# Four moves in the program's order, and sums of squares in exact bf16 parts, in a four-layer graph and expert network

## The chip, the cores and the metric

The kernel runs on one core of a Trainium2 chip. The metric is device time in microseconds (us) from start to end of one launch; lower is better. A core has four compute engines that run their own queues of instructions side by side: TensorE (PE in the profile: matmuls, and weight loads as PEld), VectorE (DVE), ScalarE (ACT) and GpSimd (POOL). SyncE (SP) issues most DMA transfers, POOL some. Each queue is executed in its order; engines wait for each other through semaphores. TensorE multiplies a stationary operand, loaded first, by a moving one.

## The reference, cut to what matters

1250 tokens of 512 features go through four layers. Each adds to x a graph part and a mixer part, both of the normed x, and then an expert part.

```python
for layer in 0..3:
    xn = layernorm(x)
    x = x + gnn[layer](xn, edges) + mixer[layer](xn)
    x = x + experts[layer](layernorm(x))

# layer 0, graph: h = xn @ W.T + b;  out[col] += dis[row]*dis[col] * h[row];  relu
# layer 0, mixer: twice an attention with random features, then an MLP
def softmax_kernel(data, proj, is_query, eps=1e-4):
    data_dash = (data * d**-0.25) @ proj.T                       # 64 -> 256 features, per head
    diag = sum(data**2, -1) * 0.5 * d**-0.5                      # the sum of squares per head
    m = max(data_dash, -1 if is_query else (-2, -1))
    return ratio * (exp(data_dash - diag - m) + eps)

# layer 1, graph: mean over neighbours @ W_l.T + xn @ W_r.T, batch norm over tokens, relu, + xn
# layer 1, mixer: linear attention, softmax over q's features
# layer 2, experts: two of eight for each token
h1 = rmsnorm(gelu(xf @ w1[e])) * n1[e]
h2 = rmsnorm(gelu(h1 @ w2[e])) * n2[e]
expert_out = (h2 + h1) @ w3[e]
# layer 3, mixer: XW_v = X @ W_v.T;  mean(XW_v over tokens) + X @ ((X @ W_theta.T).T @ XW_v) / (n*sqrt(d))
```

## The kernel before, in words

The tokens lie in 10 tiles of 125 rows; feature-major tensors (`xnT`, `kT`, `qT`) lie with 128 features on the partitions and are worked in chunks of 500, 500 and 250 tokens. `mm` writes a product of several terms to one of the PSUM banks that `bank()` gives out in turn; `transposed` turns a tile on TensorE against `ident`. The program is written in the order in which the work is wanted; a planner in the language reorders instructions on the engines by its own estimates, except those marked with `keep_in_program_order`. Pools reuse memory: what is opened later can lie where a closed pool lay, and then waits for the last readers of that memory.

Layer 0, front. `load_x` brings x in five transfers of two tiles, then `l0_front` loads W. For each tile it makes the layer norm (`ln_one`), a second norm `z` of it, turns both, and multiplies the tile before (`before`) with W; `hs` receives the product plus bias. Meanwhile `Graph.__init__` makes a tile `zero` on VectorE out of x0 (so that it waits for x) and POOL writes it in 29 DMAs over the DRAM adjacency table `adj` and a part of `yd`. x0 and `zero` lie in the pool `l0n`, which is closed after the front.

`Graph.start` makes one number (source, destination) of each edge, and `Graph.add`, 16 times, loads a row of these (`keyrow`, two buffers, on SP's queue), compares it on VectorE in ten operations `same`, and adds ten columns of counts to `adj` by indirect DMA. These groups are spread by the planner over the attention.

Layer 0, attention (`l0_attention`, run twice). Keys in four steps `keys(c)`, two heads each: project into `kT` in three chunks, square (`sq`), and sum the squares per head: a matmul with the squares as stationary operand and `halves`, a 128 x 2 constant of 0.5, as moving one. Then products with the projection `pj`, a maximum on VectorE, exponentials on ScalarE, and products with the weighted values `vw`. The pool of a keys stage, `kv`, holds `v`, `kT`, `sq`. Queries: `projected` makes `qT` and its squares a chunk ahead, `features_q` sums squares and makes features.

Layer 1. After the SAGE product (`over`), the four blocks `f` of the self product and the batch norm, `att.out` starts with `q_start` for two tiles (product with `wq`, softmax on ScalarE and VectorE), then loops over the tiles.

Layer 2, experts. A load is one expert's weight with one or two tiles of 128 slots. There are 28 loads in six groups of two stages here (`second` and `third`): for each load, scale `h` and turn it on TensorE, make `h1T` or `sT` out of that on VectorE, then multiply with w2 or w3.

Layer 3, mixer. Gram matrix of `xnT`, `half` = gram times wv in four blocks whose copies alternate between VectorE and ScalarE, then `tot`, the sum of `xnT` over tokens on VectorE, spread to `totb` and multiplied with wv for the mean. The planner is free to place `tot`; it put it ahead of the gram copies.

Of the kernel before, what the change touches and what calls it, by code (L numbers as in the profile page):

```python
# [8 lines left out]
F32 = mybir.dt.float32  # L9
# [48 lines left out]
def gps_d4_kernel(ctx: ExitStack, tc: tile.TileContext, a: dict, out: bass.AP):  # L58
# [22 lines left out]
    def load_x(engine, o):  # L81
        for t in range(0, NT, 2):
            move(engine, o[:, t:t + 2, :], a["x"][t * TP:(t + 2) * TP, :].rearrange("(t p) d -> p t d", p=TP))

    cols = const.tile([P, NCOL], F32, name="cols")
    nc.sync.dma_start(cols, a["cols"])
# [9 lines left out]
    halves = const.tile([P, 2], F32, name="halves")  # L96
# [94 lines left out]
    def ln_one(o, src, t, between=lambda: None):  # L191

        st = S.small.tile([TP, 6], F32, tag="st1", name="st1", bufs=4)
        nc.vector.bn_stats(st, src[:, t, :])
# [351 lines left out]
    class Graph:  # L546
# [4 lines left out]
        def __init__(self, pool, first, x):  # L551
            self.pool = pool
            self.next = 0

            nc.vector.tensor_scalar(first, x[:, 7:, :].rearrange("p t d -> p (t d)")[:, :T], 3e38, 0.0,
                                    op0=OP.is_gt, op1=OP.is_lt)
# [7 lines left out]
            self.count = pool.tile([TP, EC], F32, name="count")  # L564
            self.cell = pool.tile([TP, EC], I32, name="cell")
# [208 lines left out]
    def l0_front(pool, x0, xn, hs):  # L774


        w = load_w(a["L0_gnn_W"])
        b = row_bc(a["L0_gnn_b"])
        yT = xnT
        before = None  # L780
        for t in range(NT + 1):
            if t < NT:
                mv = ln_one(xn[:, t, :], x0, t)
# [7 lines left out]
                xnTt = S.small.tile([P, NC, TP], F32, tag="xnTt", name="xnTt")  # L791
                nc.scalar.copy(xnTt, transposed(xn[:, t, :]))
                gained(yT, t, transposed(z), ("L0_mix_ln1_g", "L0_mix_ln1_b", 0))
            if before is not None:
                u, m = before
                ps = bank()
                mm(ps[:TP, :], [(m[:, c, :], w[:, c, :]) for c in range(NC)])
                nc.vector.tensor_tensor(hs[:, u, :], ps[:TP, :], b[:TP, :], op=OP.add)
            before = t, xnTt
# [15 lines left out]
    RATIO = 256.0 ** -0.5  # L815

    def l0_attention(pool, i, xm, yT, front, then, aside=lambda: None):
# [17 lines left out]
        with tc.tile_pool(name=f"kv{i}", bufs=1) as kp:  # L835
# [20 lines left out]
            def keys(c):  # L856
# [6 lines left out]
                for c0, cn in CH:  # L863
                    sq = kp.tile([P, 500], F32, tag="sq", name="sq", bufs=2)
                    nc.scalar.activation(sq[:, :cn], kT[:, c0:c0 + cn], AF.Square)
                    for t, o in tiles_of(c0, cn):
                        mm(ps[:TP, 2 * t:2 * t + 2], [(sq[:, o:o + TP], halves)])
# [108 lines left out]
        with tc.tile_pool(name=f"q{i}", bufs=1) as qp:  # L976
# [4 lines left out]
            def features_q(qT, sq, at):  # L981
                psd = bank()
                for c in range(NC):
                    mm(psd[:TP, 2 * c:2 * c + 2], [(sq[:, c, at], halves)])
# [61 lines left out]
            def projected(o, c0, cn):  # L1046
                for c in range(NC):
                    proj_T(wq, c, c0, cn, o[0][:, c, :cn], "L0_mix_bq")
                    nc.scalar.activation(o[1][:, c, :cn], o[0][:, c, :cn], AF.Square)
# [5 lines left out]
            for k in range(len(CH) + 1):  # L1055
                if k < len(CH):

                    ahead.append([qp.tile([P, NC, 500], F32, tag=n, name=n, bufs=2) for n in ("qT", "sq")])
# [62 lines left out]
    def layer0_mixers():  # L1121
# [3 lines left out]
        with tc.tile_pool(name="l0a", bufs=1) as pool:  # L1125
            xn = nat(pool, "xn")
            hs = nat(pool, "hs")
            with tc.tile_pool(name="l0n", bufs=1) as lp:
                x0 = nat(lp, "x0")
                load_x(nc.sync, x0)  # L1130
                zero = lp.tile([TP, T], F32, name="zero")
                graph = Graph(gpool, zero, x0)
                yT, z = l0_front(pool, x0, xn, hs)
# [130 lines left out]
    class LinearAttention:  # L1264
# [25 lines left out]
        def out(self, pool, wq, use):  # L1290


            ready = [self.q_start(pool, t, wq) for t in range(2)]
# [88 lines left out]
    def layer1_mixers():  # L1382
        scales = dram.tile([T, 1], F32, name="scales")
        with tc.tile_pool(name="l1x", bufs=1) as pool:
# [48 lines left out]
            over(rows, False, more)  # L1433
            hT = pool.tile([P, NC, T], F32, tag="n1", name="hT")
            for f in range(NC):
                st = S.small.tile([P, 5, 6], F32, tag="bst", name="bst")
# [16 lines left out]
            rscope.close()  # L1453
# [36 lines left out]
            with tc.tile_pool(name="l1o", bufs=1) as op:  # L1490
                att.out(op, wq, use)
                arrival[1].step(NT)
# [117 lines left out]
    def layer2_ffn():  # L1610
# [4 lines left out]
        with tc.tile_pool(name="l2o", bufs=1) as op:  # L1615
# [29 lines left out]
            with tc.tile_pool(name="l2e", bufs=1) as pool:  # L1645
# [16 lines left out]
                class Group:  # L1662
# [26 lines left out]

                    def second(self):  # L1690
# [3 lines left out]
                        for i, (o, tiles) in zip(self.loads, self.at):  # L1694
# [6 lines left out]
                            for k in range(2):  # L1701
                                nc.vector.tensor_scalar(self.h1T[:, k, o * SL:(o + n) * SL], pt[:, k, :], n1[:, k:k + 1], None,
                                                        op0=OP.mult)
                            ps = bank()
# [5 lines left out]
                            for j in range(o, o + n):  # L1710
                                square(self.h2[:, j, :], ss[:, j:j + 1])
# [209 lines left out]
```

## Time and profile before

| | us |
|---|---|
| median of three runs | 3118.99 (3117.23 to 3127.1) |
| the profiled execution | 3127.68 |
| its span | 3125.7 |
| mean granted TensorE clock in it | 0.956 of full |
| TensorE busy | 2882.9 (92%) |
| VectorE busy | 1175.9 (38%) |
| ScalarE busy | 693.8 (22%) |
| POOL busy | 670.2 (21%) |

The profile shows one execution, here 8.7 us longer than the median. Its page gives busy times, 40 equal slices of the span (78 us each) in tenths, and groups of instructions by line, engine and operands; the timeline gives start and duration of each and, in brackets, how long the engine stood idle before it and what released it. L182 is the line of `mm`, L188 that of `transposed`.

### The profile page before, as it was taken

What the parts mean: (1) busy time and instruction counts of PE and PEld (TensorE: products, weight loads), DVE (VectorE), ACT (ScalarE), POOL (GpSimd) and SP (SyncE); (2) the same over time, 40 slices, a digit from 0 to 9 for tenths busy, and PEclk for the clock granted to TensorE, in tenths of its full rate; (3) what the DMA queues carried; (4) which work ended last, traced back from release to release, by engine and by line L of the source; (5) the groups of instructions that cost most, each with busy time, mean ns of one, the idle gap of its engine ahead of it and who ended that gap; (6) DMA issues with size and microseconds to landing.
All of it is one profiled execution on the core that took longest, in us unless ns stands there. A gap on an engine that the chain in (4) does not pass through costs nothing. (4 is left out here: it accounts for less than half of the span.)

```text
span 3125.7 us, 31412 instructions
## 1 busy us (share of the span) xinstructions
PE 2882.9 (92%) x11531; PEld 1724.7 (55%) x11531; DVE 1175.9 (38%) x2812; ACT 693.8 (22%) x1469; POOL 670.2 (21%) x492
## 2 busy tenths in 40 slices
PE   8999999999999999999899979999799979789884
PEld 4457744455576444656455556766454547345562
DVE  6835511143355323344531550001443135362433
ACT  3133311132233122110321431111241013230010
POOL 3444444442001300133310011000301002022023
PEclk9999999999999999999899989999899989999987
DMA  7411111121001200237310017775210026430086
GB/s 229 118 15 15 17 28 31 28 31 14 14 14 40 82 27 27 80 108 249 88 34 1 21 44 283 254 252 176 82 41 1 8 73 193 159 104 10 24 312 201
DMA packets 234382, 275.70 MB, mean 88 GB/s; under 512 B 104352, under 2 KB 131600, under 8 KB 234210
## 3 DMA queue, kind: packets, MB, share of 16 engines
q1 hardware_dynamic: 123841, 185.13, 18.3%
q0 software_dynamic: 96832, 63.67, 8.9%
q10 hardware_dynamic: 13536, 24.65, 2.1%
q8 instruction: 102, 1.67, 0.2%
q14 instruction: 71, 0.57, 0.1%
HBM read 228.04 MB, written 44.91 MB: 87 GB/s over the span
## 5 line engine op out<-in xcount | busy, mean ns | idle before, releaser
L182 PE MATMUL ps<-xnT,w 128*128 128x500 f32 (+1 forms) x1536 | 554.8, 516 | 2.9 <-PEq L698 2.3
L182 PE MATMUL ps<-w,hT 128*125 128x512 f32 (+1 forms) x1232 | 542.1, 592 | 0.9 <-ACT hT L1246 0.9
L182 PEld LDWEIGHTS ps<-xnT,w 128*128 128x128 f32 x1536 | 289.4, 190 | 252.0 <-issue 239.7
L620 POOL DMA_INDIRECT adj<-count,cell x160 | 319.7, 1998 | 369.5 <-DMA adj<-count,cell 338.1
L182 PEld LDWEIGHTS ps<-w,hT 128*125 128x125 f32 (+1 forms) x1232 | 228.9, 189 | 270.3 <-issue 260.8
L182 PE MATMUL ps<-w,xnT 128*125 128x512 f32 x560 | 254.7, 604 | 0.0
L182 PE MATMUL ps<-xgT,w 128*128 128x256 f32 (+1 forms) x1256 | 234.0, 344 | 2.8 <-issue 2.8
L182 PEld LDWEIGHTS ps<-xgT,w 128*128 128x128 f32 x1256 | 207.5, 193 | 43.5 <-issue 22.2
L378 POOL DMA_INDIRECT xg<-rows,r_idx x94 | 89.7, 955 | 571.5 <-PE ps L419 289.1
L208 DVE TENSOR_TENSOR xn<-ps,xn 125x512 f32<-125x512 f32 x100 | 69.0, 690 | 348.3 <-PE ps L182 348.3
L523 ACT ACTIVATE hT<-ps,cols 128x500 f32<-128x500 f32 (+1 forms) x108 | 65.6, 608 | 478.2 <-PE ps L182 478.1
L182 PEld LDWEIGHTS ps<-w,xnT 128*125 128x125 f32 x560 | 103.4, 192 | 115.4 <-issue 114.6
L439 POOL DMA_INDIRECT came<-yd,slots x80 | 100.5, 1256 | 302.1 <-SPq L408 136.3
L420 DVE COPY xgT<-ps 128x512 f32<-128x512 f32 x94 | 62.0, 687 | 246.3 <-PE ps L419 225.0
L182 PE MATMUL ps<-hs,AT 125*125 125x512 bf16 x600 | 134.3, 382 | 4.2 <-PEq L698 4.2
L182 PE MATMUL ps<-AT,n 125*128 125x500 bf16 (+1 forms) x720 | 127.2, 339 | 0.0
L429 DVE TENSOR_TENSOR y<-ps,erow 128x512 f32<-128x512 f32 x71 | 49.1, 692 | 194.6 <-PE ps L182 187.3
L182 PEld LDWEIGHTS <-AT 125*125 125x125 bf16 x600 | 82.0, 138 | 51.8 <-issue 7.8
L1532 ACT ACTIVATE hT<-ps,b 128x256 f32<-128x256 f32 (+1 forms) x112 | 48.8, 436 | 262.1 <-PE ps L182 262.1
L182 PEld LDWEIGHTS <-n 125*128 125x128 bf16 x720 | 70.1, 97 | 58.0 <-issue 1.1
L925 PE MATMUL ps<-ex,vw 125*65 125x256 f32 x320 | 83.3, 411 | 2.8 <-DVE vw L911 2.8
L208 DVE TENSOR_TENSOR x<-ps,x 125x512 f32<-125x512 f32 x50 | 34.5, 691 | 130.4 <-PE ps L182 117.1
(404 smaller groups left out, 3651.2 us busy)
## 6 DMA issues: line engine op xcount, KB each, us to landing
w<-in_L_ffn_we_dram SPq DMA_DIRECT2D x56, 1024.0 KB
w<-in_L_ffn_w_dram SPq DMA_DIRECT2D x58, 512.0 KB
yd<-y ACTq DMA_DIRECT2D x94, 256.0 KB
w<-in_L_mix_W_dram SPq DMA_DIRECT2D x16, 1024.0 KB
w<-in_L_ffn_w_dram SPq DMA_DIRECT2D x44, 256.0 KB
rows<-z SPq DMA_DIRECT2D x40, 224.0 KB
keyrow<-keys SPq DMA_DIRECT2D x16, 546.9 KB
erow<-in_L_ffn_b_dram SPq DMA_DIRECT2D x30, 256.0 KB
```

The costliest lines, as they stand in the source:

```text
L182: nc.tensor.matmul(o, l, r, start=(i == 0), stop=(i == n - 1))
L208: nc.vector.tensor_tensor(dst, ps, dst, op=OP.add)
L378: nc.gpsimd.indirect_dma_start(g, None, self.rows, bass.IndirectOffsetOnAxis(ap=self.idx[:, t:t + 1], axis=0))
L420: nc.vector.tensor_copy(xgT[:, :, j * SL:(j + 1) * SL], ps.rearrange("p (c s) -> p c s", c=NC))
L429: nc.vector.tensor_tensor(y, ps, bias, op=OP.add)
L439: nc.gpsimd.indirect_dma_start(y, None, yd, bass.IndirectOffsetOnAxis(ap=slots[n][:, k * NT + t:k * NT + t + 1], axis=0))
L523: nc.scalar.activation(hT[:, f, :cn], ps[:, :cn], act, bias=b1(f))
L620: nc.gpsimd.indirect_dma_start(adj, bass.IndirectOffsetOnAxis(ap=self.cell[:, c:c + 1], axis=0), self.count[:, c:c + 1], None, compute_op= ...
L925: nc.tensor.matmul(self.ps[j][:C + 1, :NB], self.vw[j][:, t, :], self.ex[k][:, j, u, :], start=(t == 0), stop=(t == NT - 1))
L1532: nc.scalar.activation(hT[f // NC][:, f % NC, :ns], ps[:, :ns], AF.Gelu, bias=b1[:, f:f + 1])
```

## The change

Five edits:

1. Front of layer 0: x comes in two single tiles, then W, then pairs of tiles, with the constants `cols` after the first pair; the product lags two tiles, and `xnTt` has three buffers; tile 2's first norm instruction is kept in program order; `zero` and the clearing of `adj` and `yd` move into `Graph.clear`, called at the sixth tile.
2. Layer 1: `q_start` for two tiles moves ahead of the last block `f`.
3. Layer 2: in `second` and `third` the next load is turned and scaled ahead of this load's product.
4. Layer 3: `tot` is kept in program order, behind the copies of `half`.
5. Layer 0, attention: each square is split into three bf16 numbers whose sum it is, and `halves` is bf16, so that a sum is three bf16 matmuls in place of one f32.

```diff
             engine.dma_start(o[r], i[r])
-    def load_x(engine, o):
-        for t in range(0, NT, 2):
-            move(engine, o[:, t:t + 2, :], a["x"][t * TP:(t + 2) * TP, :].rearrange("(t p) d -> p t d", p=TP))
+    def load_x(engine, o, tiles=range(0, NT, 2), n=2):
+        for t in tiles:
+            move(engine, o[:, t:t + n, :], a["x"][t * TP:(t + n) * TP, :].rearrange("(t p) d -> p t d", p=TP))
     cols = const.tile([P, NCOL], F32, name="cols")
-    nc.sync.dma_start(cols, a["cols"])
     ident = const.tile([P, P], F32, name="ident")
...
     nc.vector.memset(eps6, 1e-6)
-    halves = const.tile([P, 2], F32, name="halves")
+    halves = const.tile([P, 2], BF16, name="halves")
     nc.vector.memset(halves, 0.0)
...
         return ps[:, :NC * TP].rearrange("p (c t) -> p c t", t=TP)
-    def ln_one(o, src, t, between=lambda: None):
+    def ln_one(o, src, t, between=lambda: None, in_order=False):
         st = S.small.tile([TP, 6], F32, tag="st1", name="st1", bufs=4)
-        nc.vector.bn_stats(st, src[:, t, :])
+        ins = nc.vector.bn_stats(st, src[:, t, :])
+        if in_order:
+            tc.keep_in_program_order(ins)
         mv = S.small.tile([TP, 4], F32, tag="mv1", name="mv1", bufs=4)
...
-        def __init__(self, pool, first, x):
+        def __init__(self, pool):
             self.pool = pool
             self.next = 0
-            nc.vector.tensor_scalar(first, x[:, 7:, :].rearrange("p t d -> p (t d)")[:, :T], 3e38, 0.0,
-                                    op0=OP.is_gt, op1=OP.is_lt)
+            self.count = pool.tile([TP, EC], F32, name="count")
+            self.cell = pool.tile([TP, EC], I32, name="cell")
+        def clear(self, first, x):
+            tc.keep_in_program_order(nc.vector.tensor_scalar(first, x[:, 7:, :].rearrange("p t d -> p (t d)")[:, :T], 3e38, 0.0,
+                                    op0=OP.is_gt, op1=OP.is_lt))
             for t in range(NT):
...
                 nc.gpsimd.dma_start(yd[r:r + n, :], first[:n, :D])
-            self.count = pool.tile([TP, EC], F32, name="count")
-            self.cell = pool.tile([TP, EC], I32, name="cell")
         def start(self, z):
...
                 self.some()
-    def l0_front(pool, x0, xn, hs):
-        w = load_w(a["L0_gnn_W"])
+    def l0_front(pool, x0, xn, hs, w, aside):
         b = row_bc(a["L0_gnn_b"])
         yT = xnT
-        before = None
-        for t in range(NT + 1):
+        before = []
+        for t in range(NT + 2):
+            if t == 6:
+                aside()
             if t < NT:
-                mv = ln_one(xn[:, t, :], x0, t)
+                mv = ln_one(xn[:, t, :], x0, t, in_order=t == 2)
                 r = S.small.tile([TP, 2], F32, tag="r2", name="r2", bufs=4)
...
                 nc.vector.tensor_scalar(z, xn[:, t, :], r[:, 1:2], None, op0=OP.mult)
-                xnTt = S.small.tile([P, NC, TP], F32, tag="xnTt", name="xnTt")
+                xnTt = pool.tile([P, NC, TP], F32, tag="xnTt", name="xnTt", bufs=3)
                 nc.scalar.copy(xnTt, transposed(xn[:, t, :]))
                 gained(yT, t, transposed(z), ("L0_mix_ln1_g", "L0_mix_ln1_b", 0))
-            if before is not None:
-                u, m = before
+            if t > 1:
+                u, m = before[t - 2]
                 ps = bank()
...
                 nc.vector.tensor_tensor(hs[:, u, :], ps[:TP, :], b[:TP, :], op=OP.add)
-            before = t, xnTt
+            before.append((t, xnTt))
         return yT, z
...
     RATIO = 256.0 ** -0.5
+    def squares(pool, q, o, bufs=2):
+        s = pool.tile([P, 500], F32, tag="sq", name="sq", bufs=bufs)[:, :q.shape[-1]]
+        nc.scalar.activation(s, q, AF.Square)
+        nc.scalar.copy(o[:, 0, :], s)
+        nc.vector.tensor_tensor(s, s, o[:, 0, :], op=OP.subtract)
+        nc.scalar.copy(o[:, 1, :], s)
+        nc.vector.tensor_tensor(o[:, 2, :], s, o[:, 1, :], op=OP.subtract)
     def l0_attention(pool, i, xm, yT, front, then, aside=lambda: None):
...
                 for c0, cn in CH:
-                    sq = kp.tile([P, 500], F32, tag="sq", name="sq", bufs=2)
-                    nc.scalar.activation(sq[:, :cn], kT[:, c0:c0 + cn], AF.Square)
+                    sq = kp.tile([P, 3, 500], BF16, tag="sq3", name="sq3", bufs=2)
+                    squares(kp, kT[:, c0:c0 + cn], sq[:, :, :cn], 1)
                     for t, o in tiles_of(c0, cn):
-                        mm(ps[:TP, 2 * t:2 * t + 2], [(sq[:, o:o + TP], halves)])
+                        mm(ps[:TP, 2 * t:2 * t + 2], [(sq[:, k, o:o + TP], halves) for k in range(3)])
                 nc.vector.tensor_copy(half, ps[:TP, :2 * NT].rearrange("p (t h) -> p t h", h=2))
...
                 for c in range(NC):
-                    mm(psd[:TP, 2 * c:2 * c + 2], [(sq[:, c, at], halves)])
+                    mm(psd[:TP, 2 * c:2 * c + 2], [(sq[:, c, k, at], halves) for k in range(3)])
                 mx = S.small.tile([TP, H], F32, tag="qmx", name="qmx")
...
                     proj_T(wq, c, c0, cn, o[0][:, c, :cn], "L0_mix_bq")
-                    nc.scalar.activation(o[1][:, c, :cn], o[0][:, c, :cn], AF.Square)
+                    squares(qp, o[0][:, c, :cn], o[1][:, c, :, :cn])
                     yield
...
                 if k < len(CH):
-                    ahead.append([qp.tile([P, NC, 500], F32, tag=n, name=n, bufs=2) for n in ("qT", "sq")])
+                    ahead.append([qp.tile([P, NC, 500], F32, tag="qT", name="qT", bufs=2),
+                                  qp.tile([P, NC, 3, 500], BF16, tag="sq3", name="sq3", bufs=2)])
                     coming = projected(ahead[k], *CH[k])
...
                 x0 = nat(lp, "x0")
-                load_x(nc.sync, x0)
+                load_x(nc.sync, x0, range(2), 1)
+                w = load_w(a["L0_gnn_W"])
+                load_x(nc.sync, x0, range(2, 4, 2))
+                nc.sync.dma_start(cols, a["cols"])
+                load_x(nc.sync, x0, range(4, NT, 2))
                 zero = lp.tile([TP, T], F32, name="zero")
-                graph = Graph(gpool, zero, x0)
-                yT, z = l0_front(pool, x0, xn, hs)
+                graph = Graph(gpool)
+                yT, z = l0_front(lp, x0, xn, hs, w, lambda: graph.clear(zero, x0))
                 graph.start(z)
...
             return q
-        def out(self, pool, wq, use):
-            ready = [self.q_start(pool, t, wq) for t in range(2)]
+        def first(self, pool, wq):
+            return [self.q_start(pool, t, wq) for t in range(2)]
+        def out(self, pool, wq, use, ready=None):
+            ready = ready or self.first(pool, wq)
             for t in range(NT):
...
             over(rows, False, more)
+            rscope.close()
+            oscope = ExitStack()
+            op = oscope.enter_context(tc.tile_pool(name="l1o", bufs=1))
             hT = pool.tile([P, NC, T], F32, tag="n1", name="hT")
             for f in range(NC):
+                if f + 1 == NC:
+                    ready = att.first(op, wq)
                 st = S.small.tile([P, 5, 6], F32, tag="bst", name="bst")
...
                 nc.scalar.activation(hT[:, f, :], hT[:, f, :], AF.Relu, bias=g[:, 1:2], scale=g[:, 0:1])
-            rscope.close()
             b = row_bc(a["L1_mix_b_out"], late=True)
...
             arrival[1] = Arrival(1, a["L1_ffn_gw2"], hidden=hidden)
-            with tc.tile_pool(name="l1o", bufs=1) as op:
-                att.out(op, wq, use)
-                arrival[1].step(NT)
+            att.out(op, wq, use, ready)
+            arrival[1].step(NT)
+            oscope.close()
     def layer1_ffn():
...
                         self.r1 = self.means(ss[:, :self.n], "r1")
+                    def ahead(self, prepare, use):
+                        loads = [(i, *at) for i, at in zip(self.loads, self.at)]
+                        made = prepare(*loads[0])
+                        for k, load in enumerate(loads):
+                            now, made = made, prepare(*loads[k + 1]) if k + 1 < len(loads) else None
+                            use(*load, now)
                     def second(self):
...
                         ss = pool.tile([SL, GT], F32, tag="s2", name="s2", bufs=2)
-                        for i, (o, tiles) in zip(self.loads, self.at):
+                        def prepare(i, o, tiles):
                             n = len(tiles)
...
                                                         op0=OP.mult)
+                            return w2
+                        def use(i, o, tiles, w2):
+                            n = len(tiles)
                             ps = bank()
...
                                 square(self.h2[:, j, :], ss[:, j:j + 1])
+                        self.ahead(prepare, use)
                         self.r2 = self.means(ss[:, :self.n], "r2")
                     def third(self):
-                        for i, (o, tiles) in zip(self.loads, self.at):
+                        def prepare(i, o, tiles):
                             n = len(tiles)
...
                                                                self.h1T[:, k, o * SL:(o + n) * SL], op0=OP.mult, op1=OP.add)
+                            return w3, sT
+                        def use(i, o, tiles, made):
+                            w3, sT = made
                             for j, t in enumerate(tiles):
...
                                 put(pool, ps, t)
+                        self.ahead(prepare, use)
                 def use(loads, source):
...
             tot = S.small.tile([P, NC], F32, tag="tot", name="tot", bufs=1)
-            nc.vector.tensor_reduce(tot, xnT, AX.X, OP.add)
+            tc.keep_in_program_order(nc.vector.tensor_reduce(tot, xnT, AX.X, OP.add))
             totb = S.small.tile([P, NC, TP], F32, tag="totb", name="totb", bufs=1)
```

On the engines, as built, this moves the following. VectorE's instruction that makes `zero` stands behind the fourth `hs`; on VectorE, the memset of `v`, which waits for the transfers that read `zero`, and the first `kT` stand behind six groups of `same` and all ten additions `xn+=bo` (`L1040` before, `L1053` after), where one group stood before. In layer 3 the product with `totb` keeps its place on TensorE, right behind the last block of `half`; on VectorE `tot` stands behind both of its copies of `half`.

## The prediction

> **What bounds the kernel now.** I read the totals first, then the slices, then the timeline at each place that the change touches, then the waits of the layer 2 stage.
>
> ```profile
> PE 2882.9 (92%) x11531; PEld 1724.7 (55%) x11531; DVE 1175.9 (38%) x2812; ACT 693.8 (22%) x1469; POOL 670.2 (21%) x492
> ...
> PE   8999999999999999999899979999799979789884
> DVE  6835511143355323344531550001443135362433
> ```
>
> TensorE is busy 92% of a span of 3125.7 us, so a step is worth what it adds to or takes from TensorE's own time or its 8% of idle time. An instruction on another engine counts only where TensorE comes to wait for it. In the first slices VectorE is the fullest of the others (8 tenths in the second).
>
> ```profile
> 17.70 2.89 PE L182 MATMUL ps<-w,xnTt 128*125 128x512 f32 x3 [3.53 <-DMA w<-in_L_gnn_W_dram]
> ...
> 60.71 8.60 PE L182 MATMUL ps<-xnT,w 128*128 128x500 f32 x24
> 61.67 0.12 DVE L837 MEMSET v<- 125x80 f32 x1
> 61.90 0.35 DVE L614 SCALAR_TENSOR_TENSOR same<-keyrow,key,mask 125x125 f32<-125x125 f32 x1
> 62.17 0.35 DVE L614 SCALAR_TENSOR_TENSOR same<-keyrow,key,mask 125x125 f32<-125x125 f32 x1
> ...
> 64.60 0.73 DVE L831 TENSOR_SCALAR kT<-ps,cols 128x500 f32<-128x500 f32 x1
> 65.37 0.62 ACT L865 ACTIVATE sq<-kT 128x500 f32<-128x500 f32 x1 [9.68 <-DMA w<-in_L_mix_Wq_dram]
> 68.82 0.68 DVE L1040 TENSOR_TENSOR xn<-xn,row 125x512 f32<-125x512 f32 x1
> 69.14 1.80 PE L182 MATMUL ps<-halves,sq 128*125 128x2 f32 x16
> ```
>
> (Start, duration, then the instruction; idle time before it in brackets.) The first layer product waits 3.53 us for its weight; the key projections start at 60.71, and at 69.14 the sums of squares follow with no wait, because VectorE had done only one group of ten `same` operations (one each 0.27 us) before the first `kT`.
>
> ```profile
> 1740.16 0.62 PE L188 MATMUL ps<-ident,q 125*128 125x125 f32 x4 [2.90 <-DVE q L1287]
> 1740.61 5.30 PE L182 MATMUL ps<-w,xnT 128*125 128x512 f32 x8
> 1745.75 3.60 PE L182 MATMUL ps<-mix,qT 128*125 128x512 f32 x8
> ...
> PE ps L182 <- DVE sT L1724: 4.4, 6, 1.0
> PE ps L182 <- ACT h L1708: 3.9, 6, 0.8
> PE ps L182 <- DVE h1T L1702: 3.4, 6, 0.7
> PE ps L182 <- ACT y L427: 3.3, 6, 0.6
> ...
> 2799.82 5.36 DVE L1813 TENSOR_REDUCE tot<-xnT 128x4 f32<-128x5000 f32 x1 [1.00 <-ACT xnT L1772]
> 2834.17 3.60 PE L182 MATMUL ps<-w,totb 128*125 128x512 f32 x8
> 2834.37 0.69 DVE L145 COPY half<-ps 128x512 f32<-128x512 f32 x1 [6.17 <-PE ps L182]
> ```
>
> These are the stall before layer 1's queries (the product behind it takes 5.30 instead of 3.60 us), the waits of TensorE from 2600 to 2725 us (total, times, longest), and layer 3's reduction, done 29 us before its product `totb` needs it.
>
> **The change part by part.** Plus is slower. The order of the instructions on each engine comes from the two programs as built; durations come from rows of the trace.
>
> *Front of layer 0: -3.5.* The gnn weight goes out behind two single x tiles instead of behind all of x, and products lag two tiles. The first product then waits for tile 2's transposes, not for the weight: x lands at 5.7 us now and its transposes start at 9.79, so 4.1 us from landing to transpose; tile 2, queued behind the weight, should land near 10 and be turned at 14 to 15. Left are 10 products of 3.43 and 7 tiles of transposes at 0.86, 40.3 us, and about 1.5 for a slow clock: the keys start at 56 to 58 instead of 60.71. Between -2 and -5.5. `cols` and the later x tiles move behind the weight; each tile takes TensorE 4.3 us, and x came at about 300 GB/s, under 1 us a tile, so they stay ahead.
>
> *The late zero: +21.* `Graph.clear` now stands at tile 6, behind VectorE's fourth `hs`, near 33 us. Its 29 transfers on POOL's queue took from 19.05 to 56.58 to issue; at that pace they run to about 71 and land near 74. They read `zero`, and the pool of `v` and `kT` lies in memory that `zero` and x0 have left: the memset of `v` waits for them. The changed order on VectorE puts six groups of `same` (60 x 0.27 = 16.2 us), all ten `xn+=bo` (10 x 0.63 = 6.3) and the small `first` and `cell` (1.6) ahead of that memset and of `kT`, where one group stood. With t0 as the start of the key projections: key copy and `off` 0.9, those three sums, 0.7 for the first `kT` make t0 + 25.7; Square 0.62 and copy 0.58, t0 + 27; then subtract, copy, subtract with three `same` between, t0 + 29.3. TensorE ends its projections at t0 + 8.4 and has next the first sums of squares, in order. It idles 18.4 us, and 1.8 more before the second and third parts. Nothing hides this: values, features and the projections of the next keys are all queued behind it. A slow clock behind the gap adds about 1 (1.7 at 1740). ScalarE's first Square waits for the same transfers and for `kT`. VectorE gets the time back, but TensorE idled only 1 us from 62 to 140, so nothing is regained. Bounds: +14 if the adds and small operations overlap better; +32 if the loads of `keyrow` (SP, two buffers, third behind Wq and the bo row) crawl beside the zeros, or the zeros land after t0 + 36.
>
> *Layer 1, queries first: -4.6.* The 2.90 us wait goes, and 1.7 of slow product. The wait of 4.1 us at 1757.5 stays. The two q chains now sit beside the last SAGE products, and POOL has the scaled weight ready near 1609. Bounds -2.9 and -5.
>
> *Layer 2 pipelined: -17.* TensorE waited 17.2 us in that window, once for each of 28 loads; the first load of six groups has nothing ahead of it and keeps 3.7. A transpose record lasts 0.27 us although the next starts after 0.11, so each wait hides 0.16 more: 22 x 0.16 = 3.5. Sum 17. Cover: VectorE needs about 1.7 us a two-tile load, TensorE 2.2 in `second` and 3.9 in `third`. If VectorE's queue is late there, half is lost; bounds -10 and -21. The w2, w3 and column loads are issued one load earlier on SP, with four buffers.
>
> *Layer 3, `tot` in program order: +7.4.* The reduction now stands behind both of VectorE's half copies, but TensorE's order has not moved: the `totb` product follows the last half product. That copy ends at 2835.06; 5.36 of reduction and 0.41 of `totb` make 2840.9, where TensorE started at 2834.3. So 6.6 of stall, and 1.3 of clock. VectorE was free of it before: the 3.55 us stall at 2808.7 ends on `hs` of the last tile, whose own chain of five steps remains; I give 0.5 back. Bounds +5 and +9.
>
> *Squares in three bf16 parts: -3.5.* 160 f32 products go, 480 bf16 come. The row above: 16 f32 records in 1.80 us, (1.80 - 0.17)/15 = 0.109 apart, two to a product: 218 ns. The nearest bf16 row, with a stationary of 125 columns loaded for every product and at most 80 columns moving:
>
> ```profile
> 1367.51 0.71 PE L282 MATMUL ps<-r_m,onesh 125*125 125x80 bf16 x10
> ```
>
> (0.71 - 0.20)/9 = 57 ns. So 3 x 57 = 171, less 47 on 160: -7. Against it speaks the Trainium skill, "TensorE: Matmul & The Clock Gate", section "LDWEIGHTS (loading the stationary operand)": a load takes the columns over 1.2 in ns, 104 for 125 columns; unhidden, three cost 312 and the edit +15. Its section "Back-to-back issue gap" measures about 81 ns for load and matmul pairs at 128 columns moving: 243, or +4. I take the trace's row: same width of load, on this chip. Each of 48 chunks also gets two ScalarE copies (0.58) and two VectorE subtractions (0.7), some 55 us on each, beside TensorE where ScalarE shows 1 to 3 tenths; the chain from `kT` to the last part grows by about 2.6 us, and projections of later chunks cover it except at the last chunk of a step, and sums now split some pairs of feature products. For that I take +3.5. Bounds -8 and +15.
>
> Sum: -3.5 + 21 - 4.6 - 17 + 7.4 - 3.5 = -0.2 against the profiled execution's own 3127.68 us. That one lies 8.7 above the median of 3118.99 (3117.23 to 3127.1), so I put the difference on the median: 3119.
>
> **The rivals.**
> *Slower: loading the stationary sets the pace of the bf16 sums.* At the skill's 104 ns the term is +15 in place of -7: 22 more, 3141. It alone crosses the 0.3% line from about 78 ns a product, (9.4/480 = 20 ns over 57). For it: the load records last longer than the pitch. Against it: the row at 1367.
> *Slower: the zeros land late.* If they end 10 us after VectorE would be free, the stall is 31 and the time 3129.
> *Faster: the stall at the first keys is short and layer 2 gives all.* 14 for 21 and -21 for -17, and squares at -7: 3119 - 7 - 4 - 3.5 = 3104. For it: the DMA engines were over 0.8 busy only until about 50 us, so the zeros may be through early; against it: six groups stand before `kT` in the order whenever they land.
> *The change doesn't do what it says:* the front stays bound by x or by the layer norm chain and layer 2 by VectorE: +3.5 and +8, 3130.
>
> **How the numbers follow.** 0.3%, 9.4 us, is about what a measurement of this kernel can tell from no change. My sum 0.45 (3119, 3112 to 3127); faster rival 0.2; skill's load price 0.12; late zeros 0.13; not as said 0.1. Gains and losses of about 26 us each nearly cancel, so the sign is weak; the unknown costs lean to the slow side. Faster 0.22, same 0.43, slower 0.35; range 3103 to 3138.
>
> **What would show it.** TensorE idle for about 20 us behind the first key projections, ended by VectorE's `kT` and ScalarE's copy; first product near 15 us; no 2.9 us wait before `q`; layer 2 waits near 4 us; a gap of 6.6 us before `totb`; bf16 records of `halves` 57 ns apart. The forecast is wrong if the first gap is under 10 us, if layer 2 keeps its waits, or if the records stand over 78 ns apart.

## The result, and the profile after

The changed kernel takes 3146.86 us (median of five executions, 3132.42 to 3155.36), the kernel before 3121.76: a ratio of 1.0075, 95% interval 1.0052 to 1.0097. Measured again (`e1_again`) it came to 1.0103 (1.0087 to 1.0119). By these ratios it is slower by 23 to 32 us; the forecast was 3119, no change, with 3138 as its upper end.

The profiled execution is the shortest of the five: 3132.42 us, span 3130.7, only 5 us over the span of before. Its page, first the totals, then the slices:

```profile
PE 2878.4 (92%) x11691; PEld 1718.4 (55%) x11691; DVE 1223.8 (39%) x2908; ACT 746.2 (24%) x1567; POOL 667.7 (21%) x492
PE   7799999999999999999799997999799997899884
DVE  5855631143466422343541352000244135453433
```

TensorE is busy for 4.5 us less than before, VectorE for 48 and ScalarE for 52 more. TensorE's second slice has dropped to 7. The timeline of the front and the first keys (start, duration, in brackets the idle time before and what ended it):

```profile
12.86 0.72 DVE L738 TENSOR_SCALAR xnT<-ps,cols 128x125 f32<-128x125 f32 x2 [4.10 <-DMA cols<-in_cols_dram]
17.25 1.09 PE L187 MATMUL ps<-ident,xn 125*128 125x125 f32 x4 [6.47 <-DVE xn L201]
19.87 5.01 PE L181 MATMUL ps<-w,xnTt 128*125 128x512 f32 x8
...
61.80 8.60 PE L181 MATMUL ps<-xnT,w 128*128 128x500 f32 x24
76.15 0.69 DVE L1053 TENSOR_TENSOR xn<-xn,row 125x512 f32<-125x512 f32 x1 [7.46 <-DMA row<-in_L_mix_bo_dram]
94.15 0.65 DVE L844 TENSOR_SCALAR kT<-ps,cols 128x500 f32<-128x500 f32 x1
94.17 0.12 DVE L850 MEMSET v<- 125x80 f32 x1
96.20 0.27 PE L181 MATMUL ps<-halves,sq 128*125 128x2 bf16 x1 [25.80 <-ACT sq L825]
```

The first product starts at 19.87, later than before (17.70), because VectorE, which works in order, stood 4.10 us at the gain of tile 0 for `cols`, whose transfer now lies behind the weight and a pair of x tiles; tile 2's norm was queued behind. The key projections start at 61.80 (before: 60.71). Then TensorE stands 25.80 us until the first `kT` has come through VectorE's queue. The last zero transfer had issued at 70.5 and the memset did not wait when its turn came at 94.17: the order of the queue set the end, and inside that queue 7.46 us of waiting for the bo row.

Layer 1, layer 2's waits (total, times, longest, same stages as before) and layer 3:

```profile
1765.97 1.85 PE L181 MATMUL ps<-mT,w 128*128 128x250 f32 x8
1767.65 0.59 PE L187 MATMUL ps<-ident,q 125*128 125x125 f32 x4
1768.08 3.60 PE L181 MATMUL ps<-w,xnT 128*125 128x512 f32 x8
...
PE ps L181 <- ACT h L1747: 0.8, 2, 0.4
PE ps L181 <- ACT h L1707: 0.4, 1, 0.4
PE ps L181 <- DVE h1T L1737: 0.4, 1, 0.4
...
2831.26 0.69 DVE L144 COPY half<-ps 128x512 f32<-128x512 f32 x1 [6.18 <-PE ps L181]
2831.87 5.35 DVE L1860 TENSOR_REDUCE tot<-xnT 128x4 f32<-128x5000 f32 x1
2837.25 0.42 DVE L1862 TENSOR_SCALAR totb<-tot 128x500 f32<-128x500 f32 x1
2837.73 5.86 PE L181 MATMUL ps<-w,totb 128*125 128x512 f32 x8 [6.51 <-DVE totb L1862]
```

No stall is left before `q`, and the product behind takes 3.60. Of 17.2 us of waits in layer 2, 1.6 are left. The product with `totb` waits 6.51.

Setting the two traces' TensorE instructions side by side, and reading how far the second lags at the same instruction, gives a ledger of the profiled execution: front +1.1 (at the transposes of the edge numbers, 60.53 and 61.62), first key step +27.7 (lag 28.8 at the first values product), the rest of layer 0's attention and MLP +0.1, layer 1 -4.5, layer 2 and the arrival of layer 3 -23.3, layer 3's mixer +3.1 (-5.1, then +8.2 at and behind `totb`), the rest +0.8. Sum: +5.0.

The other executions of the same program are 6 to 23 us longer, at a mean granted clock of 0.949 to 0.953 where the profiled one had 0.956. So the ledger of one execution is not yet the result; the experiments say what the clock has to do with it.

### The profile page after: what moved, and what is told of

Same layout as the page of the kernel before. It is cut to its first block, busy times and chain, and to the rows that moved or that the text cites. A ratio compares the mean times of both kernels' runs of the same rounds, so it can differ in the third digit from the quotient of the medians.

```text
span 3130.7 us, 31907 instructions
## 1 busy us (share of the span) xinstructions
PE 2878.4 (92%) x11691; PEld 1718.4 (55%) x11691; DVE 1223.8 (39%) x2908; ACT 746.2 (24%) x1567; POOL 667.7 (21%) x492
## 5 line engine op out<-in xcount | busy, mean ns | idle before, releaser
L181 PEld LDWEIGHTS ps<-xgT,w 128*128 128x128 f32 x1256 | 208.2, 194 | 43.9 <-issue 22.4
```

Of the source, the lines that this page charges most:

```text
L181: nc.tensor.matmul(o, l, r, start=(i == 0), stop=(i == n - 1))
```

## The experiments

All ran beside the kernel before, and each ratio is against executions of that kernel beside it. Gains and losses in us are taken from the ratios (0.001 is 3.1 us) where two experiments did not run side by side. "Ledger" means the lag of TensorE's instructions against before, as above.

**The same kernel again.** 

> The changed kernel, unchanged. The profiled execution of it came to 3132 us, other executions of it to 3138 to 3155. Theory A (the first keys): what differs is the length of TensorE's gap behind the first key projections (25.8 us in the first profile), because in it VectorE waits for loads (the bo row, keyrow) that share the DMA engines with the late zeros; then the span less this gap stays within 3 us of 3105. Theory B: the spread is the granted clock elsewhere; then the gap is 26 us again and span less gap moves with the time.

3153.69, ratio 1.0103. The profiled execution took 3150.69. The gap behind the first key projections is the same, 26.5 us, so theory A's account of the spread falls. Up to the first product of the second attention's keys this execution lags nearly as the first one did (33.4 against 29.5 us); there, behind a wait of 0.99 us (0.61 in the first execution), it loses another 8.2 without any further gap, and 2 to 4 at three later places. Windows of 300 and 600 us of layer 0, first of the first execution, then of this one, then of the kernel before (busy us and instructions of PE, PEld, DVE, ACT, POOL; then the granted clock):

```profile
100.00:400.00 300.00, 292.25 (x1540) 190.55 (x1540) 184.07 (x529) 112.25 (x263) 144.50 (x73) 0.96 0.19 30
400.00:1000.00 600.00, 590.87 (x2400) 338.60 (x2399) 234.49 (x473) 167.06 (x353) 166.27 (x84) 0.99 0.13 23
...
100.00:400.00 300.00, 292.38 (x1521) 189.79 (x1521) 182.78 (x524) 109.05 (x254) 144.60 (x72) 0.95 0.19 30
400.00:1000.00 600.00, 590.67 (x2275) 335.24 (x2275) 223.83 (x450) 166.24 (x351) 166.91 (x84) 0.96 0.12 23
...
100.00:400.00 300.00, 291.38 (x1494) 192.30 (x1493) 166.23 (x500) 89.83 (x213) 139.93 (x70) 0.97 0.21 34
400.00:1000.00 600.00, 592.41 (x2326) 344.24 (x2325) 209.94 (x428) 142.57 (x309) 165.04 (x85) 0.97 0.14 24
```

The same busy time holds fewer instructions, and 0.03 of 600 us is 18 us, which is what the two spans differ by: theory B. What separates these two executions is the granted clock in layer 0. From 400 to 1000 us the first execution had a higher clock than the kernel before, 0.99 against 0.97.

**Clear early.** Only the place of the call moves:

```diff
-                yT, z = l0_front(lp, x0, xn, hs, w, lambda: graph.clear(zero, x0))
+                graph.clear(zero, x0)
+                yT, z = l0_front(lp, x0, xn, hs, w, lambda: None)
```

> Graph.clear back ahead of the front, all else as changed. As built, VectorE then has 20 of the operations same and 4 of the additions xn+=bo ahead of the first kT, in place of 60 and 10. Theory A (order on VectorE behind the wait for the zeros): the first kT comes near t0 + 9.5 in place of t0 + 32, TensorE's gap at the first sums of squares is 2 to 5 us and the time 3105 to 3112, below before. Rival (the three-part squares, not the clearing, make the gap): the gap stays above 15 us and the time above 3125.

3141.06, ratio 1.0056 (1.0034 to 1.0078). The gap shrank to 2.96 us as theory A said, but the time missed its 3105 to 3112: it fell by only 13 against `e1_again`. So the large gap is the clearing's, and something else costs as much.

**Zero in memory of its own, clear late.**

```diff
+            zp = zscope.enter_context(tc.tile_pool(name="l0z", bufs=1))
-                zero = lp.tile([TP, T], F32, name="zero")
+                zero = zp.tile([TP, T], F32, name="zero")
```

> Clear stays late, but the tile zero lies in a pool of its own that is closed only behind the keys, so that v and kT lie in memory that no transfer reads. As built, VectorE has 10 of the operations same and no addition ahead of the first kT, as before the change. Theory A (reused memory makes the wait and the order): gap under 3 us, 3100 to 3108. Rival (the zeros' traffic itself, beside the loads of the attention): the gap stays above 10 us although the order is that of before, 3115 or more.

3144.70, ratio 1.0063. VectorE's order is that of before, and the gap at the first sums is gone; another of 8.44 us opens inside them:

```profile
81.10 0.35 DVE L617 SCALAR_TENSOR_TENSOR same<-keyrow,key,mask 125x125 f32<-125x125 f32 x1 [8.64 <-DMA keyrow<-keys]
81.38 0.68 DVE L826 TENSOR_TENSOR sq<-sq,sq 128x500 f32<-128x500 f32 x1
82.74 0.27 PE L181 MATMUL ps<-halves,sq 128*125 128x2 bf16 x1 [8.44 <-ACT sq L827]
```

The split's subtraction is queued behind a `same` that waits for `keyrow`, whose transfer shares the DMA engines with the late zeros. The traces speak for the zeros: from 60 to 100 us VectorE waits 5.3 to 8.6 us at once for the bo row or for `keyrow` in all six traces that clear late, and for neither in any of the ten that clear early. So reuse of memory made the long order, and the zeros' traffic still makes a shorter wait: both the theory and the rival have a part. Most of the distance to theory A's 3100 to 3108 is something else, the squares, as the next runs show.

**Layer 2 alone.** 

> The kernel before with only the pipelining of layer 2's second and third. The two profiles' TensorE instructions, set side by side, put -20 to -23 us on this stage. If that is this edit's own: 3098 to 3103, ratio 0.993 to 0.995. As the prediction had it: -17, 3104. Rival (part of it is layer 3's arrival, moved by other edits): -10 to -14, 3108.

3098.22, ratio 0.9923 (0.9909 to 0.9938): 24 us, as much as was expected at most. The stage is worth some 21 in the ledger.

**All orders, no squares.** The kernel of `e3_zero_apart` with f32 sums:

```diff
-                    squares(kp, kT[:, c0:c0 + cn], sq[:, :, :cn], 1)
+                    nc.scalar.activation(sq[:, :cn], kT[:, c0:c0 + cn], AF.Square)
```

(and `halves` and the queries' sums likewise)

> The changed kernel with zero in a pool of its own (as in e3_zero_apart) and the sums of squares as f32 products again; all four moves of order stay. Theory C (the three-part squares cost by waits in the attention and by stretches of half clock behind them): TensorE's instructions run as before through layer 0's attention, the gap of 8 us at the first sums is gone, the gates lose about 130 us as in e4_only_layer2 in place of 157, and the time is 3092 to 3102, some 45 below e3_zero_apart. Rival (the orders themselves disturb the attention): 3115 to 3135.

3105.17, ratio 0.9954: by the ratios 34 us below `e3_zero_apart`, and somewhat above the 3092 to 3102 expected. The four moves of order, rid of the reused memory, gain 14 us; the squares lose about 34 on top of them. A wait of 4.90 us remains in the first key step, behind 6.25 us for the bo row: the late zeros' traffic again.

**Squares alone.** 

> The kernel before with only the squares in three parts. Theory C: 3145 to 3165, with waits of 5 to 10 us at the first sums of squares and more stretches of half clock in layer 0. As the prediction had it: -3.5, 3116 to 3120. Rival (the load of the stationary sets the pace): records of the sums 78 ns apart or more, 3135 to 3145, with no more half clock than before.

3146.76, ratio 1.0098 (1.0067 to 1.0128): 30 us by the ratio, 21 to 40 by its interval, for the edit that was forecast at -3.5. The expected wait at the first sums did not come, and the profiled execution has no more half clock than before (0.957 against 0.956; its other executions go down to 0.948). What the trace shows is the key steps after it, here and in the kernel before:

```profile
131.21 1.05 PE L182 MATMUL ps<-halves,sq 128*125 128x2 bf16 x12
132.81 0.22 PE L182 MATMUL ps<-halves,sq 128*125 128x2 bf16 x1 [0.42 <-issue]
133.92 0.34 PE L182 MATMUL ps<-g,ones 2*125 2x2 f32 x2 [0.89 <-DVE cell L618]
134.97 0.69 PE L182 MATMUL ps<-pj,kT 64*125 64x256 f32 x2
135.59 1.01 PE L182 MATMUL ps<-halves,sq 128*125 128x2 bf16 x10
...
143.68 1.13 PE L182 MATMUL ps<-pj,kT 64*125 64x256 f32 x8
144.75 1.94 PE L925 MATMUL ps<-ex,vw 125*65 125x256 f32 x8
```

Before, eight records of feature products take 1.07 us from start to next start: the two heads lie on different halves of the partitions, and their products run side by side. With sums in between, two records take 0.62. Adding up the time from each instruction's start to the next one's start over layer 0's mixers, the feature products `ps<-pj,kT` take 52.0 us before, 9.6 of them lost to half clock, and 58.4 here, 5.3 of them lost: 10.7 more without the clock. The sums themselves fall from 37.6 to 35.2.

**No squares, clear late in reused memory.** 

> The changed kernel with f32 squares, clear late and zero in the reused memory as it was changed. Theory A + C: the gap behind the first key projections stays near 24 us and gives the difference to e5_orders_no_squares of 22 to 30 us, so 3118 to 3128. Rival (without the squares the wait behind the zeros is no longer on the path): within 8 us of e5_orders_no_squares.

3131.35, ratio 1.0033: 26 above `e5_orders_no_squares` and a little above the 3118 to 3128 expected, with a gap of 26.47 us. This is the price of the reused memory under the late zeros, on its own. The changed kernel differs from this one by the squares alone: on top of the other edits they cost 13 us by its first ratio and 22 by its second.

**Two mends.** `cols` ahead of the weight; in layer 3 `graph(1)` ahead of the product with `totb`:

```diff
+                nc.sync.dma_start(cols, a["cols"])
                 w = load_w(a["L0_gnn_W"])
...
+            graph(1)
             mm(ps[:TP, :], [(totb[:, c, :], wv[:, c, :]) for c in range(NC)])
```

> e5_orders_no_squares with two mends: the constants cols loaded right behind the first two tiles of x, ahead of the gnn weight, and in layer 3 the product with totb placed behind the gather of tile 1. Expected: first layer product near 15 us in place of 19.6 and the key projections start 3 to 5 us earlier; no wait before totb, 6 to 8 us. Together 3083 to 3092. Rival for the front (x's tile 2, behind the weight, sets it): no gain there, 3090 to 3094.

3100.90, ratio 0.9938. That misses the 3083 to 3092, and is 5 us below `e5_orders_no_squares`, within the intervals. Layer 3 is mended in the trace: the gather of tile 1 now runs beside the reduction, and the mixer is 4.7 us shorter than before the change.

```profile
2798.70 6.64 PE L181 MATMUL ps<-hs,AT 125*125 125x512 bf16 x30
2799.50 5.35 DVE L1862 TENSOR_REDUCE tot<-xnT 128x4 f32<-128x5000 f32 x1
2805.36 3.70 PE L181 MATMUL ps<-w,totb 128*125 128x512 f32 x8
```

The front is not: the first product starts at 18.05, tile 2's transposes at 15.32 after a wait of 4.38. VectorE begins tile 2's norm at 12.79, after 0.47 us of waiting for x; until 12.33 it works off the gains of the tiles before. So the rival (tile 2 of x, behind the weight) was right by a narrow margin: VectorE's own queue would have allowed hardly more.

**One part, multiplied thrice.** On before, ScalarE's Square writes one bf16 number, and this enters the sum three times in place of the three parts.

> The kernel before with bf16 sums of squares, but each square rounded to one bf16 number by ScalarE's Square and that one multiplied three times: the second and third parts are left out, so the sums are coarser. TensorE has the same 480 bf16 products as in e6_only_squares; ScalarE's copies and VectorE's subtractions are gone. If the chain of five operations is what costs: 3113 to 3120, a few us under before, as the 7 us of TensorE's own saving. If the many small bf16 products cost (TensorE's own time or their effect on the clock): 3135 or more.

3101.34, ratio 0.9941 (0.9928 to 0.9954): 18 us faster, more than expected. So the 480 bf16 products do not cost, they gain. The sums fall from 37.6 to 31.4 us in the trace, and the time lost to half clock in layer 0's mixers from 32.4 to 13.7. The feature products take 46.4 us, 3.2 of them lost to half clock, no more than before: it is not the bf16 sums that break their pairs, but what comes with the split.

**The split beside.** On before, f32 sums as they were; the split's two copies and two subtractions a chunk are made and read by nothing.

> The kernel before with its f32 sums, and two ScalarE copies and two VectorE subtractions a chunk beside them whose results nothing reads: the same load on these engines as in e6_only_squares, but not between kT and TensorE. If the load on the engines is what costs (reductions and exponentials come late behind it): 3135 or more. If the place of the chain on TensorE's path costs: 3118 to 3126.

3146.26, ratio 1.0075 (1.0063 to 1.0088): 23 us with nothing added between `kT` and TensorE. So the load itself costs; the chain need not be on the path. The planner did move some of TensorE's instructions here too: the feature products take 52.6 us, 4.7 of them lost to half clock, so 5.5 more than before without the clock. The q stage of this execution, and the same stage of before in the last line, show how small delays can grow:

```profile
266.90 0.40 PE L188 MATMUL ps<-ident,ov 125*128 125x125 f32 x2 [0.90 <-DVE ov L1037]
267.87 0.43 PE L1020 MATMUL ps<-ident,qf 125*128 125x125 f32 x2 [0.57 <-ACT qf L1011]
262.00:268.00 6.00, 4.53 (x39) 3.90 (x36) 5.67 (x14) 1.26 (x3) 3.89 (x2) 1.00 0.08 2
268.00:288.00 20.00, 20.00 (x78) 15.44 (x79) 6.70 (x14) 5.87 (x16) 9.90 (x5) 0.52 0.11 2
...
257.00:279.00 22.00, 22.00 (x168) 18.47 (x167) 14.42 (x34) 7.10 (x18) 10.81 (x6) 1.00 0.12 2
```

Two waits of 0.90 and 0.57 us, and then 20 us at a clock of 0.52 with TensorE busy all the time: some 10 us lost behind 1.5 us of waiting. Before, TensorE did not wait in this stage and had the full clock.

**Which engine's load.** 

> The kernel before with its f32 sums and two ScalarE copies a chunk beside them that nothing reads. If the load on ScalarE (copies between the exponentials and the copies of ct) is what costs the 25 us of e10_split_beside: 3138 to 3148. If it is VectorE's: 3118 to 3128.

> The kernel before with its f32 sums and two VectorE subtractions a chunk beside them that nothing reads. If the load on VectorE (71 of 80 us busy in the first keys) is what costs: 3138 to 3148. If it is ScalarE's: 3118 to 3128. Half each would say that both queues delay the same small operations that TensorE waits for.

The copies alone: 3126.11, ratio 1.0020 (1.0010 to 1.0030), 6 us. The subtractions alone: 3136.37, ratio 1.0049 (1.0029 to 1.0068), 15 us, a little under the 3138 expected. Together they make nearly the 23 of `e10_split_beside`; VectorE's share is the larger. The second key step shows how it comes about, with the subtractions and then before:

```profile
128.26 0.67 DVE L820 TENSOR_TENSOR sq<-sq 128x500 bf16<-128x500 f32 x1
128.85 0.67 DVE L821 TENSOR_TENSOR sq<-sq 128x500 bf16<-128x500 f32 x1
130.25 0.73 DVE L837 TENSOR_SCALAR kT<-ps,cols 128x500 f32<-128x500 f32 x1
131.74 1.22 PE L182 MATMUL ps<-halves,sq 128*125 128x2 f32 x8 [2.29 <-ACT sq L871]
135.33 2.08 PE L182 MATMUL ps<-pj,kT 64*125 64x256 f32 x8
...
129.78 0.74 DVE L831 TENSOR_SCALAR kT<-ps,cols 128x500 f32<-128x500 f32 x1 [0.66 <-PE ps L182]
131.27 1.80 PE L182 MATMUL ps<-halves,sq 128*125 128x2 f32 x16
134.34 1.13 PE L182 MATMUL ps<-pj,kT 64*125 64x256 f32 x8
```

Before, VectorE waited for TensorE's projection and TensorE took its sums without a wait. Here VectorE is busy with subtractions and `same`, and the second `kT` comes after them. TensorE, which is 2.7 us ahead of before at this point, waits 2.29 us for its square, and the feature products behind it run at half clock. From 60 to 1000 us TensorE waits 22.4 us here and 15.4 before.

**The best combination.** Before with layer 2, layer 1 and the mended layer 3; front, clearing and squares as before.

> The kernel before with layer 2's pipelining, layer 1's queries first, and in layer 3 tot behind the half copies with its product behind the gather of tile 1; front, clearing and squares as before. Expected from the stages: 25 from layer 2, 4.6 from layer 1, 5 to 6 from layer 3, so 3084 to 3090, ratio 0.988 to 0.990. Rival (the gains overlap in the stretches of half clock): 3092 to 3098.

3092.97, ratio 0.9898 (0.9880 to 0.9915): 32 us faster than before and 54 faster than the changed kernel. That is less than the stages promised, and in the range of the rival.

> e11_best with each square rounded to one bf16 number and multiplied once: 160 bf16 products in place of 160 f32 ones, nothing added on the other engines; the second and third parts are left out, so the sums are coarser. By TensorE's own time 160 x (218 - 57) = 26 us less than e11_best, by e9_one_part_thrice some 13 us more than that again from fewer stretches of half clock: 3054 to 3068. If the gain of e9_one_part_thrice was all clock: 3075 to 3080.

3061.76, ratio 0.9813 (0.9792 to 0.9834), 27 us below `e11_best` by the ratios, 31 by the medians. In the traces the sums take 24 us less (13.0 for 37.1), the mean clock rises from 0.957 to 0.962, and TensorE's waits from 60 to 1000 us rise from 14.5 to 21.4, 7.4 of them for `sq`; so part of what the clock gives back is lost in waits. Its sums have one bf16 part of each square.

## Why the prediction was wrong, by its own steps

- **Squares, -3.5: the step that failed.** Alone they cost 30 us, and 13 to 22 on top of the other edits. TensorE's own pitch was right: ten records of bf16 sums take 0.74 us at full clock, (0.74 - 0.20)/9 = 60 ns apart, near the 57 of the row at 1367 and not the 104 estimated for a load of 125 columns from the Trainium skill, "TensorE: Matmul & The Clock Gate", section "LDWEIGHTS (loading the stationary operand)"; of the 7 us that this was to bring, the sums gave 6.2 without the split (`e9_one_part_thrice`) and 2.4 with it (`e6_only_squares`). So the slower rival fell by its mechanism, though it had the sign. What failed is "some 55 us on each, beside TensorE where ScalarE shows 1 to 3 tenths". I read the cover from ScalarE, and from slices of 78 us over the whole stage. VectorE counts more: its subtractions alone cost 15 us, ScalarE's copies alone 6. In the first keys VectorE was busy 70.92 of 80 us before the change, and the `kT` that TensorE's sums wait for passes its queue. The added load costs 23 us with no product changed. The other part is the broken pairs of feature products, some 11 us in `e6_only_squares`, which I had inside a +3.5 together with the chain. Some 5 of these come with the load too, so the two do not simply add up, and how the 30 divide is known only roughly.
- **Late zero, +21: right in mechanism, too small.** The first key step lost 27.7 in the ledger, 26 between two kernels. The term I left at its likelier value was the wait for the bo row, 7.46 us beside the zeros; my bounds (+14 to +32) held it.
- **Front, -3.5: wrong sign, +1.1.** The sum followed TensorE and the weight, and had tile 2 turned at 14 to 15. It was turned at 17.25: `cols`, moved behind the weight, held VectorE's queue. With `cols` early it was still 15.32: x came only at 12.79, where I had it near 10.
- **Layer 1, -4.6:** -4.5.
- **Layer 2, -17:** some 21 in the stage and 24 in the time. The waits fell from 17.2 to 1.6, so also those of the first loads, which I had kept at 3.7, went; that the load of the group before covers them is likely, not shown.
- **Layer 3, +7.4:** the wait was 6.51 for 6.6. But moving the reduction gave back 5.1 where I had 0.5: the stall of 3.55 at 2808.7 fell to 0.15 with the slow clock behind it. I had taken the last tile's chain as five steps that stay; it had waited for VectorE, which was behind by the reduction.
- **The sum.** The ledger of the profiled execution ends at +5, near the forecast, but that is luck: behind the first key step layer 0 shows +0.1 with the squares in it, because this execution had the higher clock there (0.99 against 0.97 from 400 to 1000 us). Without the squares the other edits come to +10 (`e7_no_squares_late`), where I had them at +3.3. The rest of the +25 of the medians is the squares, by waits, by broken pairs and by the granted clock, for which I had one us behind each gap.

## What to carry to other kernels

Work put on an engine "beside" the bottleneck is free only where that engine's queue has room at that place: read the busy time in the window of the stage, for every engine that the edit loads and not for the emptier one alone. When a transfer that reads a tile is made later, look at what reuses the tile's memory and at what a planner then puts ahead of the waiting instruction. An instruction moved on one engine needs its consumer moved on the other: the same reduction lost 6.5 us in front of its product and gained 4.7 once a gather stood between.

## What the runs showed of the hardware

- Small waits can be followed by a loss of many times their length, by the clock. The Trainium skill, "TensorE: Matmul & The Clock Gate", section "What's actually happening", has the clock halved after an idle window of some 3.4 us, and whole again after one busy window. Here 0.90 and 0.57 us of idle time were followed by 20 us at 0.52, with TensorE shown as busy in all of them. The measurement decides: no idle time of 3.4 us came first, and a stretch that the profile shows as busy did not bring the full clock back. Small waits don't always do this: at the same place in two executions of the changed kernel 0.99 us was followed by half clock, and 0.61 was not. What decides is not shown.
- The same program's executions differ by up to 23 us in their span at granted clocks from 0.949 to 0.956 (the changed kernel). Other kernels spread less: 9 us for `e9_one_part_thrice` (0.961 to 0.964), 6 for `e4_only_layer2` (0.957 to 0.961). One profiled execution can hide the result, as here.
- Feature products of 64 partitions, two heads on the two halves, ran side by side only where they stood next to each other in TensorE's queue: 1.07 us for eight records against 0.62 for two.
- Still open: why the time lost to half clock falls by 19 us with the bf16 sums alone. TensorE's saving doesn't explain it, and no run here takes it apart.
